# Dealing out the x products of a block by columns: 320, fourteen times 290, and 324 a step

## The chip, the cores and the metric

The kernel runs on one core of one Trainium2 chip. The metric is the time of one execution in device microseconds; for the kernel before, three runs were taken.

## The reference

The kernel computes a gated recurrence over 512 time steps for a batch of 8, with 512 inputs and 512 hidden units, and adds its input:

```python
def step(h, x_t):
    fused = jax.nn.sigmoid(jnp.concatenate([x_t, h], axis=-1) @ w_W + w_b)
    hidden_state, output_state = jnp.split(fused, 2, axis=-1)
    memory_state = x_t @ wx_W + wx_b + hidden_state * (h @ wh_W + wh_b)
    h_new = output_state * h + (1.0 - output_state) * jnp.tanh(memory_state)
    return (h_new, h_new)
_, hs = jax.lax.scan(step, h0, xT)
x = x + swapaxes(hs, 0, 1)
```

Each step needs the h of the step before. The parts that multiply x_t do not depend on h; they can be computed ahead for many steps at once. Everything is float32.

## The kernel before

**Steps.** One loop runs over the 512 steps. In each step TensorE first multiplies h, in the order `A0 A1 A2 A3 D0 D1 D2 D3 H2 H3` (`ORDER`): a letter is a PSUM bank (A 256 columns, D 128, H 64), a digit is one of four chunks of 128 hidden units. A2 and A3 use 192 of A's columns. For each of them four matmuls of 32 output columns go to four strips of the array (`j`, partitions 32j to 32j + 31). All matmuls go through the helper `mm`, so their line in the profile is always L203. The state h lies in `hT`, in two halves: chunks 0 and 1, and chunks 2 and 3.

When A is complete, VectorE transposes the gates out of it (`turn_r`, whose tile is `tr`, L523, then `turn_h`, `turn_z`, `turn_part`), ScalarE applies the sigmoids and the tanh, and VectorE's scans (L511) form the memory state `m` and, in `update`, the new `hT`: first the half that A0 and A1 of the next step read, then the half that A2 and A3 read. VectorE also has three short memsets on `idle` to settle its order.

**The x side.** The 512 steps make 32 blocks of 16 (`TC`). The x part of the first two blocks is computed directly (`prefill`). From the third block on it comes out of a two-level fast multiplication, which needs 49 products a block instead of 64: seven stages `STAGES` of seven products. Each product is `BL` = 96 columns wide, with four `mm` for the four strips; each `mm` is recorded in the trace as two matmuls with two weight loads. The stationary operand is a 128 x 32 piece of x or of sums of x (`xin`, `so`, `si`), the moving one a 96-column piece of weights or of differences of weights (`wx`, `tw`, `ti`).

A stage puts three products side by side into PSUM bank `xps[0]` (columns 0 to 287) and four into `xps[1]` (0 to 383); `SLOTS` says which. When a bank is complete in a stage, VectorE adds it to earlier sums (`drain`, L403), and the next stage writes that bank again, in some stages accumulating on what stands there. GpSimd adds up the results (`result`) and also forms the sums of x.

**What sets the order.** All orders are written out by hand (`manual_schedule`): instructions of an engine run in the order in which the Python code emits them. `products` is a generator that yields after each product, `x_side` chains it over blocks 2 to 31, and the loop over steps advances it with `take` right after the matmuls of H, so the x products of a step stand between H of this step and A0 of the next. `LEAD` = 18 makes the products of block c run from step 16c - 18 on. The number of products per step is in

```python
take(later, 4 if (i + LEAD) % TC == TC - 1 else 3)
```

which gives 15 steps of three and one of four: 49. A second loop, ahead of the steps, counts the same numbers (`done += 3 + w // 15`) and lists for each step the drains of the banks that are complete by then; VectorE runs them at the end of that step, after the updates. The last 18 steps have no x products.

Of the kernel before, what the change touches and what calls it, by code (L numbers as in the profile page):

```python
# [14 lines left out]
NQ = 4  # L15
# [19 lines left out]
BL = 96  # L35
# [3 lines left out]
FRESH = (2, 5, 1)  # L39

SLOTS = ((1, 6, 7), (2, 3, 4, 5))

LEAD = 18

PLAIN = (2, 3, 5, 6, 8, 10, 11, 13, 14, 16)

# [8 lines left out]
def tile_cond_rnn_residual(  # L55
# [144 lines left out]
    xps = [psum.tile([P, 512], F32, name=f"xp{q}") for q in range(2)]  # L200

    def mm(out_, lhsT, rhs, start=False):
        nc.tensor.matmul(  # L203
            out_, lhsT, rhs, start=start, stop=False, skip_group_check=True
        )
# [20 lines left out]
    for b in range(2):  # L226
        c0 = COLS.start + BL * b
# [56 lines left out]
    def wx_of(kh, nh):  # L284
        return wx[:, 2 * kh : 2 * kh + 2, :, HALF * nh : HALF * nh + HALF]
# [31 lines left out]
    def x_block(c, r, kh):  # L317

        return xins[c][:, :, 2 * kh : 2 * kh + 2, 32 * r : 32 * r + 32]
# [31 lines left out]
    def x_sums(c):  # L351
        jobs = [(x_sum, c, n) for n in range(4)]
        return jobs + [(inner_x, c, n, p) for n in range(4) for p in (0, 2, 3)]

    def left(c, p, q):

        xr, kh = {1: (0, 0), 2: (0, 1), 4: (1, 1)}.get(p, (None, None))
        at = {1: 0, 2: 1, 4: 2, 5: 3, 6: 4, 7: 5, 3: 6}[p]
        if q in (3, 5, 6, 7):
            return si[c % 2][:, at, {5: 0, 6: 1, 7: 2, 3: 3}[q]]  # L360
        e, k = {1: (0, 0), 2: (0, 1), 4: (1, 1)}[q]
        if xr is None:
            return so[c % 2][:, at - 3, e, k]
        return x_block(c, xr, kh)[:, e, k]

    def right(p, q, j):

        kh, nh = {1: (0, 0), 2: (1, 0), 3: (1, 1)}.get(p, (None, None))
        at = {1: 0, 2: 1, 3: 2, 5: 3, 6: 4, 7: 5, 4: 6}[p]
        if q > 3:  # L370
            return ti[:, at, {5: 0, 6: 1, 7: 2, 4: 3}[q], j]
        k, b = {1: (0, 0), 2: (1, 0), 3: (1, 1)}[q]
        w = tw[:, at - 3] if kh is None else wx_of(kh, nh)
        return w[:, k, j, BL * b : BL * b + BL]

    def products(c):

        for q in STAGES:
            for bank in range(2):
                for n, p in enumerate(SLOTS[bank]):  # L380
                    for j in range(NQ):
                        mm(
                            xps[bank][32 * j : 32 * j + 32, BL * n : BL * n + BL],
                            left(c, p, q),
                            right(p, q, j),
                            start=q in FRESH and n == 0,
                        )
                    yield

    def drain(q, bank):  # L390

# [28 lines left out]
    def take(it, n=None):  # L420
        while n is None or n > 0:
            if next(it, it) is it:
                return
            n = None if n is None else n - 1

    def x_side():
        for c in range(2, NCH):
            yield from products(c)
# [4 lines left out]
    later = x_side()  # L433
# [13 lines left out]
    def at_step(i, *todo):  # L447
        jobs.setdefault(i, []).extend(todo)
# [7 lines left out]
    for c in range(2, NCH):  # L456
        w0 = TC * c - LEAD
        for n, q in enumerate(x_sums(c)):
            at_step(w0 - (13 if c > 2 else 10) + n // 2, q)
        done = 0  # L460
        for w in range(TC):
            n = done
            done += 3 + w // 15
            for m, q in enumerate(STAGES):
                for bank in range(2):
                    if n < 7 * m + 3 + 4 * bank <= done:
                        drains.setdefault(w0 + w, []).append((q, bank))
        for e, w in ((0, 11), (1, 15)):
            for n in range(7):
                at_step(w0 + w + n // 2, (result, e, n))  # L470

    pool_done = {}
    for i in range(T):
        g, s = divmod(i, GS)
        c, t = divmod(i, TC)
# [6 lines left out]
        for n in (ORDER if i else FIRST).split():  # L482
# [3 lines left out]
            bank, k = n[0], int(n[1])  # L486
# [10 lines left out]
        if 1 <= i < 4:  # L497
            take(first[2], 2 if i == 3 else 3)
        elif i == 0:
            take(first[1], 1)  # L500
        elif i < 4 + len(PLAIN):
            take(first[4], PLAIN[i - 4] - (PLAIN[i - 5] if i > 4 else 0))
        else:
            take(later, 4 if (i + LEAD) % TC == TC - 1 else 3)

        rows = slice(B * s, B * s + B)
        s1 = (i + 1) % GS
# [253 lines left out]
```

## Time and profile before

| | |
|---|---|
| median of three runs | 1645.9 us (1644.61 to 1647.66) |
| the profiled execution | 1646.05 us, span 1644.0 us |
| PE busy | 1628.2 us, 53006 matmuls |
| PEld busy | 1360.1 us, 53006 weight loads |
| DVE busy | 1379.4 us |
| ACT busy | 976.8 us |
| POOL busy | 569.3 us |
| mean granted TensorE clock | 1.000 |

How to read it: the span goes from the first to the last instruction of one profiled execution. PE is TensorE's matmuls, PEld its weight loads, which overlap with matmuls; DVE is VectorE, ACT ScalarE, POOL GpSimd. The end of a matmul is modelled, so a busy PE isn't PE at its peak. In a timeline row stand the start, the duration, the engine, the line, the operation, out<-in, the shape and the count of merged instructions, and in brackets the idle time of the engine before it with what ended it. In a row of windows stand the stretch, its length, and for PE, PEld, DVE, ACT and POOL the busy time and count, then the granted clock, the DMA share and GB/s. In a row of waits stand the total, the number and the longest, in microseconds. In a group by shape stand the busy time in us and the mean of one instruction in ns.

### The profile page before, as it was taken

How to read it: one execution, taken by the hardware profiler on the slowest of the kernel's cores; microseconds unless marked ns; L12 is line 12 of the kernel's file. 1: busy time of each engine (PE TensorE's matmuls, PEld its weight loads, DVE VectorE, ACT ScalarE, POOL GpSimd, SP SyncE). 2: the span in 40 equal slices, each digit the busy share in tenths (PEclk: the TensorE clock that was granted, in tenths of full speed). 3: DMA queues.
4: the chain of work that ended last, by engine and by line, in shares of the span. 5: the costliest groups of instructions: out<-in, count | busy, mean ns of one | idle time of the engine just before them, and what ended most of it. 6: DMA issues, size and time to landing. Idle time of an engine off the chain costs nothing.

```text
span 1644.0 us, 124813 instructions
## 1 busy us (share of the span) xinstructions
PE 1628.2 (99%) x53006; PEld 1360.1 (83%) x53006; DVE 1379.4 (84%) x11215; ACT 976.8 (59%) x5520; POOL 569.3 (35%) x1467
## 2 busy tenths in 40 slices
PE   8999999999999999999999999999999999999998
PEld 4788888888888888888888888888888888888876
DVE  8688888888888888888888888888888888888886
ACT  3666656556555656666656656655655566666665
POOL 7433333333333333333333333333333333333220
PEclk9999999999999999999999999999999999999999
DMA  4000000000000000000000000000000000000000
GB/s 181 11 10 18 18 18 17 6 18 17 18 18 5 18 18 18 18 17 5 18 18 18 18 5 18 18 18 17 18 5 18 18 18 18 5 18 11 12 11 10
DMA packets 11512, 31.08 MB, mean 19 GB/s; under 512 B 1220, under 2 KB 1732, under 8 KB 10952
## 3 DMA queue, kind: packets, MB, share of 16 engines
q1 hardware_dynamic: 10800, 22.94, 4.1%
q8 instruction: 414, 6.78, 1.7%
q14 instruction: 146, 1.20, 0.2%
q10 hardware_dynamic: 152, 0.16, 0.0%
HBM read 14.70 MB, written 8.39 MB: 14 GB/s over the span
## 4 chain that ended last, share of the span: by engine, by line
PE 97%; DVE 2%; POOL 1%; DMA 0%; issue 0%; ACT 0%; DVEq 0%; POOLq 0%
PE A L203 48%; PE D L203 26%; PE xp L203 16%; PE H L203 7%; DVE tr L523 0%; DVE m L511 0%; POOL ti L315 0%; DMA rows<-in_bias_dram 0%; DVE hT L511 0%; POOL xs L225 0%; DVE md1B L580 0%; DVE md1A L538 0%; DVE tz L523 0%; POOL off L229 0%; DVE tw L296 0%
## 5 line engine op out<-in xcount | busy, mean ns | idle before, releaser
L203 PE MATMUL A<-wa,hT 128*32 128x256 f32 x16352 | 885.9, 356 | 5.7 <-DVE hT L511 5.2
L203 PEld LDWEIGHTS A<-wa,hT 128*32 128x32 f32 x16352 | 507.7, 123 | 241.4 <-DVE hT L511 138.9
L203 PE MATMUL D<-wd,hT 128*32 128x128 f32 x16384 | 543.1, 273 | 1.0 <-DMA wd<-in_wd_dram 1.0
L203 PEld LDWEIGHTS D<-wd,hT 128*32 128x32 f32 x16384 | 482.8, 122 | 21.7 <-DMA wd<-in_wd_dram 1.3
L675 POOL TENSOR_TENSOR ot<-xin,hT 128x32 f32<-128x32 f32 x503 | 132.3, 263 | 1047.3 <-DVE hT L511 1035.9
L243 ACT ACTIVATE hT<-m 128x8 f32<-128x8 f32 x2048 | 324.4, 207 | 98.0 <-DVE m L511 97.7
L243 ACT ACTIVATE md0A<-tr 128x16 f32<-128x16 f32 x512 | 112.9, 220 | 407.3 <-DVE tr L523 407.3
L523 DVE STREAM_TRANSPOSE tr<-A 128x64 f32<-128x64 f32 x511 | 127.7, 250 | 229.1 <-PE A L203 229.1
L243 ACT ACTIVATE hT<-hT 128x16 f32<-128x16 f32 x1024 | 233.1, 228 | 85.0 <-DVE hT L511 84.2
L203 PE MATMUL H<-wa,hT 128*32 128x64 f32 x8208 | 210.3, 219 | 0.0
L203 PEld LDWEIGHTS H<-wa,hT 128*32 128x32 f32 x8208 | 187.5, 122 | 0.0
L511 DVE TENSOR_TENSOR_SCAN hT<-hd0A,hT 128x24 f32<-128x24 f32 x1024 | 176.3, 172 | 0.0
L511 DVE TENSOR_TENSOR_SCAN hT<-hd0B,hT 128x24 f32<-128x24 f32 x1024 | 154.4, 192 | 21.8
L511 DVE TENSOR_TENSOR_SCAN m<-md0B,md1B 128x24 f32<-128x24 f32 x1024 | 154.5, 192 | 0.0
L203 PE MATMUL xp<-ti,si 128*32 128x96 f32 x5040 | 150.1, 246 | 0.2 <-issue 0.2
L511 DVE TENSOR_TENSOR_SCAN m<-md0A,md1A 128x16 f32<-128x16 f32 x1024 | 144.2, 182 | 5.1
L243 ACT ACTIVATE md0B<-tr 128x16 f32<-128x16 f32 x512 | 116.2, 227 | 42.2 <-DVE tr L523 0.5
L418 POOL TENSOR_TENSOR xs<-ff 128x192 f32<-128x192 f32 x240 | 140.6, 596 | 0.2
L580 DVE STREAM_TRANSPOSE md1B<-A 128x64 f32<-128x64 f32 x511 | 130.0, 254 | 0.0
L243 ACT ACTIVATE hd0A<-tz 128x16 f32<-128x16 f32 x512 | 116.6, 228 | 21.4
L538 DVE STREAM_TRANSPOSE md1B<-H 128x64 f32<-128x64 f32 x512 | 127.8, 250 | 0.0
L573 DVE STREAM_TRANSPOSE hd0B<-sz 128x64 f32<-128x64 f32 x512 | 126.4, 247 | 0.0
(103 smaller groups left out, 1924.4 us busy)
## 6 DMA issues: line engine op xcount, KB each, us to landing
xin<-in_x_dram SPq DMA_DIRECT2D x31, 256.0 KB, 3.3
out_dram<-ot SPq DMA_DIRECT2D x31, 256.0 KB, 2.2
wx<-in_wx_dram SPq DMA_DIRECT2D x4, 768.0 KB, 7.1
wa<-in_wa_dram SPq DMA_DIRECT2D x4, 512.0 KB, 9.7
wd<-in_wd_dram SPq DMA_DIRECT2D x1, 768.0 KB
wd<-in_wd_dram SPq DMA_DIRECT2D x1, 256.0 KB, 11.2
out_dram<-ot SPq DMA_DIRECT2D x1, 192.0 KB, 1.8
head<-in_xh_dram ACTq DMA_DIRECT2D x1, 144.0 KB, 5.1
```

What stands on the lines that cost most here:

```text
L203: nc.tensor.matmul(out_, lhsT, rhs, start=start, stop=False, skip_group_check=True)
L243: inst = nc.scalar.activation(out_, in_, func, **kw).ins
L418: nc.gpsimd.tensor_tensor(to, a, b, ALU.add)
L511: return nc.vector.tensor_tensor_scan(*[t_[:, :, c_].rearrange("p n c s -> p (n c s)") for t_ in (out_, d0, d1)], 0.0, ALU.mult, ALU.add,).ins
L523: inst = nc.vector.transpose(t_.rearrange("p c n -> p (c n)"), raw[n][hf]).ins
L538: inst = nc.vector.transpose(md1[hf][g % 2][:, :, :, hf].rearrange("p n c -> p c n"), raw["h"][hf]).ins
L573: inst = nc.vector.transpose(hd0[1][i % 2][:, :, :, 2].rearrange("p n c -> p c n"), sz).ins
L580: nc.vector.transpose(md1[1][g % 2][:, :, :, 0].rearrange("p n c -> p c n"), ps["A"][:, :HU])
L675: pool_done[i + 1] = nc.gpsimd.tensor_tensor(ot[:, t], x_of(c, slice(0, NQ), t, 1), hTs[(i + 1) % NH][:, :, :, B * s1 : B * s1 + B, 2].rea ...
```

## The change

The x products are no longer dealt out in whole products but in columns. A block has 49 x 96 = 4704 columns; `BURSTS` gives 320 to the first step of a block, 290 to each of the next fourteen, and 324 to the last. Where a burst ends inside a product, the product is divided: its first columns are multiplied in this step and the rest in the next, with the same stationary operand loaded again. A divided product that opens a bank marks only its first piece as the start. The generator now yields after each burst, so a step takes one. The list of drains counts columns instead of products.

```diff
+BURSTS = (320,) + (290,) * 14 + (324,)
...
     def products(c):
 
+        todo = list(BURSTS)
         for q in STAGES:
             for bank in range(2):
                 for n, p in enumerate(SLOTS[bank]):
-                    for j in range(NQ):
-                        mm(
-                            xps[bank][32 * j : 32 * j + 32, BL * n : BL * n + BL],
-                            left(c, p, q),
-                            right(p, q, j),
-                            start=q in FRESH and n == 0,
-                        )
-                    yield
+                    c0 = 0
+                    while c0 < BL:
+                        c1 = min(BL, c0 + todo[0])
+                        for j in range(NQ):
+                            mm(
+                                xps[bank][32 * j : 32 * j + 32, BL * n + c0 : BL * n + c1],
+                                left(c, p, q),
+                                right(p, q, j)[:, c0:c1],
+                                start=q in FRESH and n == 0 and c0 == 0,
+                            )
+                        todo[0] -= c1 - c0
+                        c0 = c1
+                        if not todo[0]:
+                            todo.pop(0)
+                            yield
...
-            done += 3 + w // 15
+            done += BURSTS[w]
             for m, q in enumerate(STAGES):
                 for bank in range(2):
-                    if n < 7 * m + 3 + 4 * bank <= done:
+                    if n < BL * (7 * m + 3 + 4 * bank) <= done:
                         drains.setdefault(w0 + w, []).append((q, bank))
...
-            take(later, 4 if (i + LEAD) % TC == TC - 1 else 3)
+            take(later, 1)
```

## The prediction

> **What bounds the kernel now.** The page first: its span, its busy line and the instruction queue; then the waits of the whole run.
>
> ```profile
> span 1644.0 us, 124813 instructions
> PE 1628.2 (99%) x53006; PEld 1360.1 (83%) x53006; DVE 1379.4 (84%) x11215; ACT 976.8 (59%) x5520; POOL 569.3 (35%) x1467
> PEld A L203 <- DVE hT L511: 138.9, 489, 1.4
> DVE tr L523 <- PE A L203: 229.1, 510, 1.5
> ```
>
> PE is busy 99%, which looks like a TensorE-bound kernel. The two waits say otherwise: 489 times, about once in each of the 512 steps, the weight load of A waits for the scan that makes hT, and 510 times VectorE waits for A. Two engines that wait for each other once a step form a loop, and either side of it can set the pace. So I read one step of three products in the timeline, from one transpose `tr` (VectorE's first work once A is complete) to the next.
>
> ```profile
> 801.55 1.06 PE L203 MATMUL D<-wd,hT 128*32 128x128 f32 x32
> 801.80 0.25 DVE L523 STREAM_TRANSPOSE tr<-A 128x64 f32<-128x64 f32 x1 [0.31 <-PE A L203]
> 802.42 0.41 PE L203 MATMUL H<-wa,hT 128*32 128x64 f32 x16
> 802.65 0.35 PE L203 MATMUL xp<-wx,xin 128*32 128x96 f32 x8
> 802.81 0.51 PE L203 MATMUL xp<-tw,so 128*32 128x96 f32 x16
> 803.14 1.73 PE L203 MATMUL A<-wa,hT 128*32 128x256 f32 x32
> 803.74 0.20 DVE L511 TENSOR_TENSOR_SCAN hT<-hd0B,hT 128x24 f32<-128x24 f32 x1
> 804.00 0.51 PEld L203 LDWEIGHTS A<-wa,hT 128*32 128x32 f32 x16 [0.28 <-DVE hT L511]
> 804.94 0.25 DVE L523 STREAM_TRANSPOSE tr<-A 128x64 f32<-128x64 f32 x1 [0.41 <-PE A L203]
> ```
>
> VectorE starts at 801.80 and its scan of the second half of hT ends at 803.94; 0.06 us later the load for the last half of A goes out, having sat idle 0.28 us; A then needs until 804.94. The x products run from 802.65 to 803.14, while PE would otherwise wait for VectorE. They are filler, and they cost time only once they are longer than the hole.
>
> How deep the hole is shows in the windows over fifteen steps of three products, one step of four, and sixteen steps near the end that have no x products at all; under them the same windows for the tile xp, then the starts of `tr` that I used as borders, then the steady stretch of thirty blocks.
>
> ```profile
> 779.87:826.87 47.00, 47.00 (x1572) 39.52 (x1565) 39.99 (x328) 28.30 (x161) 16.53 (x44) 1.00 0.05 16
> 826.87:830.14 3.27, 3.27 (x124) 2.89 (x117) 2.78 (x22) 1.93 (x11) 0.87 (x4) 1.00 0.02 5
> 1585.69:1635.72 50.03, 46.19 (x1292) 35.39 (x1285) 36.54 (x333) 29.82 (x170) 7.50 (x22) 1.00 0.04 13
> ...
> 1585.69:1635.72 50.03, 0.00 (x0) 0.00 (x0) 0.00 (x0) 0.00 (x0) 1.00 0.04 13
> ...
> 779.87 0.25 DVE L523 STREAM_TRANSPOSE tr<-A 128x64 f32<-128x64 f32 x1 [0.44 <-PE A L203]
> 826.87 0.25 DVE L523 STREAM_TRANSPOSE tr<-A 128x64 f32<-128x64 f32 x1 [0.41 <-PE A L203]
> 830.14 0.25 DVE L523 STREAM_TRANSPOSE tr<-A 128x64 f32<-128x64 f32 x1 [0.44 <-PE A L203]
> 1585.69 0.25 DVE L523 STREAM_TRANSPOSE tr<-A 128x64 f32<-128x64 f32 x1 [0.44 <-PE A L203]
> 1635.72 0.25 DVE L523 STREAM_TRANSPOSE tr<-A 128x64 f32<-128x64 f32 x1 [0.88 <-PE A L203]
> ...
> 74.26:1585.69 1511.43, 1510.98 (x50172) 1278.76 (x50165) 1283.03 (x10501) 908.86 (x5160) 513.37 (x1359) 1.00 0.05 15
> ```
>
> Three products: 47.00 / 15 = 3.133 us a step. Without x products: 50.03 / 16 = 3.127 us, the same within 6 ns though a sixth of PE's work is missing. So the step of three products goes at the pace of the loop through VectorE. Four products: 3.27 us, and PE is the slower side there:
>
> ```profile
> 828.30 1.41 PEld L203 LDWEIGHTS A<-wa,hT 128*32 128x32 f32 x32
> ```
>
> all 32 loads of A in one row, with no wait for hT. A block of sixteen steps thus takes 15 x 3.133 + 3.270 = 50.265 us. Thirty such blocks are 1507.9 us; the steady stretch has 1511.43, so 3.5 us go to other stalls (below).
>
> **What a column and a split cost PE.** The mean duration of one matmul by shape:
>
> ```profile
> L203 PE MATMUL H<-wa,hT 128*32 128x64 f32 x8208 | 210.3, 219 | 0.0
> L203 PE MATMUL xp<-wx,xin 128*32 128x384 f32 x192 | 17.9, 486 | 0.0
> ```
>
> (486 - 219) / 320 = 0.834 ns a column. One product is eight recorded matmuls (the 802.65 row), that is, two passes of four strips that run side by side. A step of four products has 28 passes: A eight (four of 256 and four of 192 columns), D eight of 128, H four of 64, x eight of 96, 3840 columns together. 3840 x 0.834 = 3.203 us; the 0.067 us missing to 3.27 are 2.4 ns a pass. So a pass of n columns takes 0.834 n + 2.4 ns, a piece of a product two passes, and a split by itself 4.8 ns, if its weights arrive in time. Three products: 3648 columns and 26 passes, 3.105 us. The hole has 3.133 - 3.105 = 0.028 us left, and four products miss it by 0.137 us.
>
> **The change, part by part.** Columns per block stay 4704. The borders between steps fall 32, 34 and so on to 60 columns into a product, never on its edge, so a block has 15 pieces more: 450 in thirty blocks. Every burst consists of four pieces.
>
> - First step, 320 columns: 32 columns and one piece more, 53.4 + 4.8 = 58 ns, PE 3.163 us: 30 ns longer than 3.133.
> - Fourteen steps of 290: 3.3 + 4.8 = 8 ns, PE 3.113 us, still 20 ns inside the hole: nothing. What hides them is the wait for the hT scan; without that cover they would cost 14 x 8 = 114 ns a block.
> - Last step, 324 columns: 36 columns and one piece more than three products, 65 ns, PE 3.170 us instead of 3.270: 100 ns gained.
>
> Sum: 70 ns a block, 2.1 us in thirty.
>
> No other engine's order changes. Stage ends lie at columns 288, 672, 960 and so on, and each falls into the same step as before, so every drain keeps its step and none meets another. A bank 1 is written again 288 columns after its last drain point; a burst of 290 could overrun that only if it began one column ahead of a stage end, and all borders are even. So PE gets no new wait for a drain that is late. SP, ScalarE and GpSimd issue what they did.
>
> **Short pieces.** A pass cannot be shorter than the loading of the next weights. The shortest passes now are H's 64 columns: four in 802.42 to 802.65, 57 ns each, near the formula's 56, so a load fits into 56. The new pieces have 32 to 64 columns, down to 29.1 ns. Nearest to a bound from below is the load that came late, cut off by two windows that end 10 ns apart:
>
> ```profile
> 804.00 0.14 PEld L203 LDWEIGHTS A<-wa,hT 128*32 128x32 f32 x4 [0.28 <-DVE hT L511]
> 804.00 0.17 PEld L203 LDWEIGHTS A<-wa,hT 128*32 128x32 f32 x5 [0.28 <-DVE hT L511]
> ```
>
> At 804.03 four loads have started, at 804.04 a fifth: the second set follows the first by 30 to 40 ns. I take 35, since this is a load as fast as it goes, and H only shows that it isn't slower than 56. Passes under 35 ns are those under 39 columns. In the middle steps the 20 ns of room cover them (34 columns: 2 x (35 - 30.8) = 8). The first step pays 2 x (35 - 29.1) = 12 ns for its piece of 32, the last 2 x (35 - 32.4) = 5 for its piece of 36. That takes 17 of the 70 ns: 53 a block, 1.6 us.
>
> The Trainium skill, page "TensorE: Matmul & The Clock Gate", section "LDWEIGHTS (loading the stationary operand)", puts a load at its number of columns divided by 1.2 GHz, 27 ns for 32 columns. By it, no piece would be short of weights and the sum would stay at 2.1 us; the trace's 30 to 40 ns are above it, and I go by the trace.
>
> **More instructions to fetch.** From the page and from the waits of the weight loads in the window 75 to 1586:
>
> ```profile
> q8 instruction: 414, 6.78, 1.7%
> PEld A L203 <- issue: 1.2, 2, 0.6
> PEld xp L203 <- issue: 0.6, 2, 0.4
> ```
>
> 6.78 MB over 106,012 PE records are 64 bytes each, so q8 feeds PE. The 450 pieces add 16 records each, 7200, 6.8%: 28 more packets. In the steady stretch four waits, 1.8 us, have no releaser but issue; I take them, and the rest of the 3.5 us, for late fetches. In proportion they grow by 0.24 us. A packet comes every 1644 / 414 = 3.97 us and then every 3.72, so each late one is 0.25 us later: 1 us for four. Bounds 0 and 2 (half of 3.5 more); I take 0.4.
>
> Together: -1.6 + 0.4 = -1.2 us. The profiled execution took 1646.05 us (2.05 outside its span, untouched); it comes to 1644.85. It lies 0.15 above the median of the runs, which goes from 1645.9 to 1644.7 us. That is 0.07%; a measurement of this kernel tells about 0.2%, 3.3 us, from no change, so this is a forecast of no measurable difference.
>
> **Rivals.**
>
> Short pieces hold PE up (slower). If a pass needs 56 ns whatever its columns, each middle step has a leading and a trailing piece, 98 columns together, and pays 2 x (112 - 86.5) = 51 ns: 3.164 us, 31 over the loop, fourteen times. First step 3.217 (84 more than now), last 3.217 (53 less). 434 + 84 - 53 = 465 ns a block, +13.9 us: 1659.8. At 45 ns a pass the change breaks even; at 50 the middle steps pay 9 ns on average, first and last +72 and -65, 139 ns a block, +4.2 us: 1650.1. It decides from just under 50 ns. For it: nothing shorter than 56 was ever sustained here. Against: the 30 to 40 ns above. Chance 0.22.
>
> Everything fits (faster). If PE's sums for the two ends were too high and all sixteen steps ran at 3.133, 137 ns a block go, 4.1 us: 1641.8. The late fetches can help too: their 3.5 us may fall elsewhere when packets meet other steps. Against: the formula leaves 30 and 37 ns in the two ends. With the scatter of three runs (1644.61 to 1647.66) 0.20.
>
> The change doesn't do what it says: PE sets the pace in the steps of three as well, so evening out gains nothing and 450 splits cost 4.8 ns each, +2.2 us: 1648.1. The stretch without x products speaks against it. Chance 0.05. Late fetches at their upper bound with the rest as forecast, 1646.3: 0.10, also without measurable difference.
>
> **How the numbers follow.** The forecast itself has 0.43; its own range is 1643.5 (nothing for short pieces or fetches, and some scatter) to 1646.5. The rival of short pieces lies beyond 3.3 us slower in all of its 0.22, and scatter and late fetches add 0.04: slower 0.26. Faster 0.20 is the rival alone. Same: 0.43 + 0.05 + 0.10 less the 0.04, 0.54. The range for 8 in 10 runs from 1642.2, near the fastest case, to 1652, a pass of some 51 ns.
>
> **What would show it.** In the profile after: fourteen of sixteen `tr` to `tr` distances at 3.13 us; 3.16 to 3.18 in the two ends, no 3.27; weight loads of A still waiting for hT some 480 times, with a shorter total; matmuls of xp from 32 columns up whose group starts lie at 0.834 n + 2.4 ns a pass, not under about 35; DVE, ACT and POOL counts unchanged; q8 near 442 packets. Passes of 50 ns or more for short pieces, middle steps above 3.14, or many more issue waits would prove it wrong.

## The result, and the profile after

The changed kernel takes 1700.21 us (median of four runs, 1691.68 to 1706.29) against 1646.45 before: a ratio of 1.0319 (95% interval 1.03 to 1.0338), 3.2% slower. The forecast was 1644.7 us, no measurable difference.

The page of the changed kernel; its profiled execution took 1695.39 us:

```profile
span 1693.2 us, 132013 instructions
PE 1662.4 (98%) x56606; PEld 1432.5 (85%) x56606; DVE 1385.3 (82%) x11215; ACT 976.9 (58%) x5520; POOL 570.5 (34%) x1467
q8 instruction: 442, 7.24, 1.8%
```

The counts are as worked out: 3600 more matmuls and as many loads, 28 more packets on the instruction queue, nothing new on DVE, ACT and POOL. Busy time on DVE grew by 6 us only. What grew is time in which PE has nothing to do. The waits of the weight loads in the window 75 to 1630 (total, times, longest), and under them those for hT in the kernel before, window 75 to 1586:

```profile
PEld A L205 <- DVE hT L521: 89.2, 360, 0.6
PEld xp L205 <- issue: 21.7, 55, 0.6
PEld A L205 <- issue: 8.2, 21, 0.6
PEld H L205 <- issue: 4.0, 13, 0.5
PEld D L205 <- issue: 1.8, 8, 0.3
...
PEld A L203 <- DVE hT L511: 120.9, 442, 0.4
```

Before, issue (a wait for nothing that the profile shows) stood behind four loads and 1.8 us in the steady stretch; now behind 97 loads and 35.7 us, and not in front of the divided xp products alone but also of A, H and D, whose instructions did not change. The waits for hT have become fewer, 360 instead of 442. A wait that also strikes tiles whose instructions are unchanged doesn't look like a wait for the data of divided products. The timeline of the weight loads, in a bad stretch:

```profile
770.68 0.27 PEld L205 LDWEIGHTS H<-wa,hT 128*32 128x32 f32 x8
771.40 0.19 PEld L205 LDWEIGHTS H<-wa,hT 128*32 128x32 f32 x8 [0.46 <-issue]
...
774.62 0.18 PEld L205 LDWEIGHTS xp<-wx,xin 128*32 128x32 f32 x8
775.15 0.16 PEld L205 LDWEIGHTS xp<-wx,so 128*32 128x32 f32 x8 [0.34 <-issue]
...
778.89 0.15 PEld L205 LDWEIGHTS xp<-ti,si 128*32 128x32 f32 x7 [0.31 <-issue]
...
782.91 0.94 PEld L205 LDWEIGHTS A<-wa,hT 128*32 128x32 f32 x23 [0.61 <-DVE hT L521]
```

and the windows from the end of one of these gaps to the end of the next (length, then busy time and count of PE, PEld and the others):

```profile
771.39:775.14 3.75, 3.54 (x128) 2.93 (x128) 2.87 (x24) 2.01 (x13) 0.90 (x3) 1.00 0.02 4
775.14:778.89 3.75, 3.65 (x128) 3.05 (x128) 2.54 (x25) 2.04 (x13) 0.75 (x3) 1.00 0.02 7
778.89:782.91 4.02, 3.84 (x128) 3.26 (x128) 3.32 (x28) 2.19 (x13) 0.97 (x3) 1.00 0.01 4
```

128 matmuls and 128 loads lie between two gaps, each time. 256 recorded instructions of 64 bytes are 16 KB, one packet of q8. (The last gap is put down to hT, but it falls on the same count of 256; part of it at least is of the same kind.) Counted record by record, all 97 issue waits of the window stand at one place in the count: the load that waits is number 92 of each 128 near the start and number 78 near the end, moving evenly and never more than half a load off. (A few instructions of PE that aren't among the records would explain the movement; that isn't shown.) The four waits of the kernel before stand at the same place to within a load. PE stops where a packet of its program ends and goes on 3.75 to 4.02 us after it last went on. That gives the theory: **PE's program arrives no faster than one packet in some 3.7 us**, whatever the instructions do. A step before had 208 recorded PE instructions, 208 / 256 x 3.7 = 3.01 us, hidden under the loop's 3.133; the change makes it 224, which need 3.24 us, and that no longer fits (both times are estimates from the 3.7 us).

The steady stretch gives the mean. In thirty blocks of the changed kernel, from the `tr` of step 14 to that of step 494:

```profile
74.31:1634.61 1560.30, 1543.75 (x53772) 1351.09 (x53765) 1288.50 (x10501) 908.75 (x5160) 514.60 (x1358) 1.00 0.05 15
```

53772 + 53765 records are 420.1 packets, 3.71 us each. Before, by the row of that stretch, 50172 + 50165 records in 1511.43 us were 391.9 packets, 3.86 us each: only 4% above 3.71, and the change asked for 7% more instructions.

### The profile page after: what moved, and what is told of

Read it like the earlier page. It is cut to its first block, busy times and chain, and to the rows that moved or that the text cites. A ratio compares the mean times of both kernels' runs of the same rounds, so it can differ in the third digit from the quotient of the medians.

```text
span 1693.2 us, 132013 instructions
## 1 busy us (share of the span) xinstructions
PE 1662.4 (98%) x56606; PEld 1432.5 (85%) x56606; DVE 1385.3 (82%) x11215; ACT 976.9 (58%) x5520; POOL 570.5 (34%) x1467
## 4 chain that ended last, share of the span: by engine, by line
PE 96%; DVE 2%; issue 1%; POOL 1%; ACT 0%; DVEq 0%; POOLq 0%
PE A L205 47%; PE D L205 25%; PE xp L205 16%; PE H L205 7%; DVE tr L533 0%; DVE m L521 0%; POOL ti L317 0%; DVE hT L521 0%; DVE md1B L590 0%; DVE md1A L548 0%; DVE tz L533 0%; POOL xs L227 0%; POOL off L231 0%; DVE tw L298 0%; DVE md1B L548 0%
## 5 line engine op out<-in xcount | busy, mean ns | idle before, releaser
L205 PE MATMUL A<-wa,hT 128*32 128x256 f32 x16352 | 907.5, 356 | 7.8 <-DVE hT L521 5.2
L205 PEld LDWEIGHTS A<-wa,hT 128*32 128x32 f32 x16352 | 560.7, 124 | 195.1 <-DVE hT L521 107.9
L205 PE MATMUL D<-wd,hT 128*32 128x128 f32 x16384 | 565.4, 273 | 1.1 <-DMA wd<-in_wd_dram 0.9
L205 PEld LDWEIGHTS D<-wd,hT 128*32 128x32 f32 x16384 | 504.7, 122 | 18.2 <-issue 1.8
L205 PE MATMUL H<-wa,hT 128*32 128x64 f32 x8208 | 235.2, 219 | 2.2 <-issue 1.9
L205 PEld LDWEIGHTS H<-wa,hT 128*32 128x32 f32 x8208 | 208.4, 122 | 4.5 <-issue 4.0
L205 PE MATMUL xp<-ti,si 128*32 128x96 f32 (+12 forms) x6480 | 166.2, 229 | 3.7 <-issue 3.2
L205 PEld LDWEIGHTS xp<-ti,si 128*32 128x32 f32 x6480 | 136.6, 110 | 6.5 <-issue 6.0
```

The lines of the kernel that those rows point to most:

```text
L205: nc.tensor.matmul(out_, lhsT, rhs, start=start, stop=False, skip_group_check=True)
```

## The experiments

Theory 1 is the supply of instructions, theory 2 that the divided or short products cost the time themselves, by their passes or by their waits. The kernels ran on three chips, each beside runs of the kernel before: D0 divided, the change with a merged H, half a packet and three divided products a block beside 19 runs (median 1645.87 us); those of 240, 216 and 192 and the one with A0 divided beside 13 (1646.54); one divided product a block beside 15 (1646.23). In brackets stand the ratio to the kernel before on the same chip and its 95% interval.

**As many instructions without any divided product** (the kernel before, changed in the loop over `ORDER`):

```diff
-            for j in range(NQ):
-                mm(to[32 * j : 32 * j + 32, :], hs, w_[:, k, j])
+            w = to.shape[1]
+            halves = ((0, w // 2), (w // 2, w)) if bank == "D" and k == 0 and 14 <= i < 494 else ((0, w),)
+            for u0, u1 in halves:
+                for j in range(NQ):
+                    mm(to[32 * j : 32 * j + 32, u0:u1], hs, w_[:, k, j, u0:u1])
```

> The kernel before, whole x products, but in steps 14 to 493 the D0 matmuls are issued as two halves of 64 columns: 16 more recorded PE instructions a step (208 becomes 224), 4.8 ns more of PE work, nothing shorter than 64 columns. Theory 1, instruction supply (PE gets 256 recorded instructions, one 16 KB packet, no faster than about every 3.75 us, so a step of 224 needs 3.28 us against a loop of 3.13): as slow as the changed kernel, 1685 to 1715 us, with long gaps on PE at packet borders. Theory 2, the short and divided x products themselves are slow: no change, 1645 to 1649 us.

Measured: 1707.31 us (1.0376, 1.0359 to 1.0393). The x products are those of the kernel before, and the time is that of the change or a little more. Theory 2 falls here: no divided product is needed for the slowdown. The window over its steady stretch:

```profile
74.02:1645.97 1571.95, 1554.59 (x54008) 1352.31 (x54001) 1296.35 (x10500) 907.88 (x5160) 513.82 (x1359) 1.00 0.05 15
```

**The change with 16 instructions fewer.** H2 and H3, two matmuls of 64 columns per strip, become one of 128:

```diff
-BANKS = {"A": 256, "D": 128, "H": 64}
+BANKS = {"A": 256, "D": 128, "H": 128}
...
+            one = bank == "H" and 14 <= i < 494
+            if one and k == 3:
+                continue
...
-                "H": (ps["H"], wa[:, :, :, :64]),
+                "H": (ps["H"], wa[:, :, :, :128]) if one else (ps["H"][:, :64], wa[:, :, :, :64]),
```

> The changed kernel with all its divided products, but in steps 14 to 493 H2 is one matmul of 128 columns per strip and H3 is left out: the same PE columns, 16 recorded PE instructions fewer a step (224 becomes 208). H3's share of the sum is left out. Theory 1, instruction supply: the stalls go and the gain first forecast shows, 1643 to 1647 us. Theory 2, divided products are slow in themselves or wait for drains: still about 1700 us.

Measured: 1641.75 us (0.9976, 0.9967 to 0.9985), 58 us below the changed kernel with all its divided products in place, and below the range expected. All waits of its weight loads in the window 75 to 1586:

```profile
PEld A L205 <- DVE hT L524: 126.1, 483, 0.4
```

The window over its steady stretch:

```profile
74.65:1581.06 1506.41, 1506.41 (x49932) 1273.07 (x49924) 1283.53 (x10501) 908.90 (x5160) 513.59 (x1358) 1.00 0.05 15
```

One kind of wait is left, the one for hT, and not one issue. This kernel also shows what the rest of the prediction was worth. Its timeline of PE in a first step of a block:

```profile
828.81 0.51 PE L205 MATMUL xp<-tw,so 128*32 128x96 f32 x16
829.14 0.24 PE L205 MATMUL xp<-wx,xin 128*32 128x32 f32 x8
829.20 1.06 PE L205 MATMUL A<-wa,hT 128*32 128x256 f32 x16
```

The timeline of DVE at the `tr` starts around that first step and around a last one:

```profile
827.80 0.25 DVE L536 STREAM_TRANSPOSE tr<-A 128x64 f32<-128x64 f32 x1 [0.34 <-PE A L205]
830.99 0.25 DVE L536 STREAM_TRANSPOSE tr<-A 128x64 f32<-128x64 f32 x1 [0.45 <-PE A L205]
874.85 0.25 DVE L536 STREAM_TRANSPOSE tr<-A 128x64 f32<-128x64 f32 x1 [0.41 <-PE A L205]
878.02 0.25 DVE L536 STREAM_TRANSPOSE tr<-A 128x64 f32<-128x64 f32 x1 [0.33 <-PE A L205]
```

The piece of 32 columns takes 829.14 to 829.20, two passes of 30 ns; it is 60 ns in each of the thirty blocks. First step 3.19 us here and last 3.17 (means over thirty blocks 3.18 and 3.17; forecast 3.175 for both), and the thirty blocks take 1506.41 us where the forecast's 50.212 a block makes 1506.36. That the two agree to 0.05 us is partly luck: the merged H also saves two passes a step, by the forecast's formula 4.8 ns in the first and in the last step, 0.3 us in thirty blocks.

**Half a packet of other instructions ahead of the loop** (in the changed kernel):

```diff
     mm(xps[1], zeros[:, :128], zeros, start=True)
+    for _ in range(32):
+        mm(xps[1][:, :8], zeros[:, :128], zeros[:, :8])
```

> The changed kernel with 32 matmuls of 8 zero columns ahead of the loop, 128 recorded PE instructions, half a packet. A step has 224 instructions, seven eighths of a packet, so packet borders fall at the same place of a step every eight steps; half a packet moves them by four steps. Theory 1, instruction supply: the slow steps, in the change the burst numbers 0, 1, 2 and 8, 9, 10 of a block, become 4, 5, 6 and 12, 13, 14; total again 1690 to 1710 us. Theory 2, the cost sits in certain pieces or stages: the slow steps stay where they are.

Measured, one run: 1723.83 us, above the range, because the 32 matmuls weren't hidden: step 14 begins at 89.10 us instead of 74.31. Without these 14.8 us it is 1709.0. Mean step in us by its number in the block, counted from step 14 on and worked out from the starts of `tr` in all thirty blocks:

```
step in block     0    1    2    3    4    5    6    7    8    9   10   11   12   13   14   15
before         3.13 3.13 3.13 3.21 3.14 3.13 3.14 3.13 3.14 3.13 3.13 3.14 3.14 3.13 3.14 3.27
changed        3.39 3.34 3.41 3.14 3.13 3.16 3.21 3.23 3.39 3.37 3.34 3.14 3.14 3.15 3.19 3.29
shifted        3.18 3.15 3.15 3.55 3.46 3.49 3.28 3.16 3.14 3.16 3.16 3.22 3.39 3.44 3.38 3.18
```

The slow steps were 0 to 2 and 8 to 10 and are now 3 to 5 and 12 to 14, half a period on (3 to 4 steps, where 4 were expected), though each step has the same pieces as before. The period is eight steps, since 224 is seven eighths of 256. Why some steps are slow and others not can be estimated: from one border to the next are one step and 32 records more, 16 matmuls. Sixteen of H take 0.23 us (802.42 to 802.65 in the kernel before), so PE would be at the next border after 3.133 + 0.23 = 3.36 us and must wait for a packet that takes 3.7. Sixteen of A with 256 columns take by the formula four passes of 216 ns, 0.86 us; PE is there after 3.99 us and the packet has come.

**How the cost grows with the count.** D0 and D1 divided as D0 was above (240 a step), D0 divided only in even steps (216), A0 divided instead of D0 (224, with the new instructions among the longest matmuls), and the kernel before with the merged H of the second experiment (192; H3's share left out). The conditions in `halves` are

```text
240: bank == "D" and k < 2 and 14 <= i < 494
216: bank == "D" and k == 0 and 14 <= i < 494 and i % 2 == 0
224: bank == "A" and k == 0 and 14 <= i < 494
```

> The kernel before with D0 and D1 issued as two halves of 64 columns in steps 14 to 493: 240 recorded PE instructions a step, 10 ns more PE work. Theory 1, instruction supply at about 3.7 to 3.8 us per 256: 240 of them need 3.47 to 3.56 us a step against 3.14, so 480 steps cost 160 to 200 us more: 1805 to 1850 us. Rival, only the place of a packet border in the step matters and supply in total is enough: a cost like that of 224, about 1700 us, or less.

> The kernel before with D0 issued as two halves of 64 columns in every second step of 14 to 493: 216 recorded PE instructions a step on average. Theory 1, instruction supply: 216 need 3.13 to 3.2 us, just at the loop's 3.133, so the onset: 1648 to 1675 us. Rival, cost in proportion to added instructions (61 us for 16 a step): 1676 us.

> The kernel before with A0, the longest matmul, issued as two halves of 128 columns in steps 14 to 493: 224 recorded PE instructions a step as in the change, but the 16 more lie among long matmuls, not among short ones. Theory 1 as a matter of the mean rate: 1690 to 1715 us. Rival, only the density of instructions around the short matmuls matters: under 1660 us.

> The kernel before with H2 as one matmul of 128 columns per strip and H3 left out in steps 14 to 493: 192 recorded PE instructions a step, the same PE columns. H3's share of the sum is left out. Theory 1, instruction supply: the 3.5 us of stalls that the kernel before still has go, its pace of 15 x 3.133 + 3.265 stays: about 1642.5 us, so that the dealing out by columns, which gave 1641.75 at 208 instructions, is worth only 1 to 2 us. Rival, the kernel before has no stalls of supply: 1645.9 us, and all 4 us of that run came from the dealing out.

Measured: 1803.01 us for 240 (1.0952, 1.093 to 1.0974), 1657.91 for 216 (1.0068, 1.0051 to 1.0085), 1693.07 for A0 (1.0284, 1.0263 to 1.0304), 1644.31 for 192 (0.9988, 0.9979 to 0.9997). The first three speak for theory 1: 240 a hair under its range of 1805 to 1850, far above a cost that depends on the border's place alone; 216 at the onset, below the proportional 1676; A0 inside 1690 to 1715 and far from the rival's 1660, so the count decides in the main. Whether the place of the instructions adds something stays open: with the same count, A0 divided is 14 us faster than D0 divided, but the two ran on different chips, and the four runs of the changed kernel alone are 14.6 us apart. The steady stretch of 240:

```profile
74.55:1743.76 1669.21, 1607.58 (x57848) 1396.45 (x57841) 1312.03 (x10500) 913.78 (x5160) 514.15 (x1359) 1.00 0.05 14
```

of 216:

```profile
75.13:1597.94 1522.81, 1519.54 (x52088) 1298.22 (x52081) 1286.15 (x10500) 914.84 (x5160) 514.21 (x1359) 1.00 0.05 15
```

with A0 divided:

```profile
74.02:1632.27 1558.25, 1545.20 (x54004) 1391.33 (x53997) 1289.25 (x10501) 915.04 (x5160) 514.00 (x1359) 1.00 0.05 15
```

and of 192:

```profile
74.06:1583.17 1509.11, 1509.11 (x46332) 1268.13 (x46326) 1283.91 (x10500) 914.39 (x5160) 514.06 (x1359) 1.00 0.05 15
```

Records divided by 256, and the length by that: 3.69 us a packet at 240, 3.74 at 216, 3.69 with A0 divided, 3.73 with D0 divided, 3.71 in the change, 3.75 with half a packet ahead of the loop (53774 + 53766 records in 1574.36 us), 3.86 before and in the second experiment, 4.17 at 192. Wherever PE is short of program, the packet costs about the same 3.7 us, and at 208 a step and below the loop decides.

The kernel of 192 came out 2.2 us under the one before, not the 3.4 expected, and 1.8 us above its 1642.5; still under the rival's 1645.9. Its steady stretch is 2.3 us shorter than before, so most, not all, of the 3.5 us of other stalls was supply. That fits the kernel before: 2.2 us of them lie in four single steps of 3.40 to 3.86 us, all of them number 3 of their blocks, and that number has 3.14 us in the kernel of 192.

**Fewer divided products, all of the work kept.** Twelve steps of 288 and then four that share the rest; and fourteen of 288 with 336 twice:

```diff
-BURSTS = (320,) + (290,) * 14 + (324,)
+BURSTS = (288,) * 12 + (320, 300, 300, 328)
```

> The changed kernel with other bursts: 288 columns in the first twelve steps of a block, then 320, 300, 300 and 328, so that only three products a block are divided (3392 recorded PE instructions a block, against 3344 before and 3584 in the change). PE's own work by 0.834 ns a column and 2.4 ns a pass: 3.163, 3.130, 3.130, 3.177 us in the last four steps, against 3.133 three times and 3.270: 63 ns a block less, 1.9 us. Theory 1, instruction supply: 212 instructions a step on average stays within 256 per 3.75 us, but the last four steps have 224, so some stalls: 1643 to 1649 us. Theory 2, a divided product costs by itself (54 us for 450 of them, 0.12 us each): 90 of them, 1656 us.

```diff
-BURSTS = (320,) + (290,) * 14 + (324,)
+BURSTS = (288,) * 14 + (336, 336)
```

> The changed kernel with bursts of 288 in fourteen steps and 336 in the last two: one divided product a block, 3360 recorded PE instructions (3344 before). PE's work in the last two steps 3.19 us each, against 3.133 and 3.27 before: 23 ns a block, 0.7 us less. Theory 1, instruction supply: two steps in a row of 224 instructions instead of one may give a few more stalls; 1645 to 1648 us, no difference that can be measured, and no version that keeps all the work gets to the 1642 us seen with 16 instructions fewer. Rival, an even load is what counts and a few divided products are free: 1645.2 us or less.

Measured: 1648.36 us (1.0015, 1.0005 to 1.0024) with three divided products a block, 1646.27 (0.9999, 0.999 to 1.0008) with one. Even three in a block give back more than the 1.9 us that they gain on PE, and one gains nothing that shows; its interval, 1.6 us down to 1.3 us up, doesn't shut out the 0.7 us that the rival forecast. Theory 2's price of 0.12 us for each divided product (1656) fails again.

No version that computes everything beat the kernel before. The second experiment suggests what it would take: the columns dealt out as in the change, and 16 recorded PE instructions fewer a step from somewhere. I found no place for that which doesn't put work ahead of a bank that VectorE waits for.

## Why the prediction was wrong

**The step that failed** is "More instructions to fetch". It foresaw the 7200 records and the 28 packets, and it priced them at 0.4 us with 2 as the upper bound. Measured: the steady stretch of the changed kernel is 1560.30 us, 53.9 above the 1506.4 that its pace without stalls makes, against 3.5 before. The term was 50 us. I treated late packets as four accidents that grow in proportion. They were the first signs of a floor. The 3.97 and 3.72 us a packet that I compared are means over the whole run, and the start and the last 18 steps thin them out. In the steady stretch the forecast's 50.212 us a block for 14 packets ask for one every 3.59 us, and 3.71 on average, with 3.75 to 4.02 in a row of gaps, is what PE gets: 14 x 30 times the 0.12 to 0.13 us between them is the loss. The trace of before doesn't hold the floor, but it holds a bound that I didn't draw: its steady row gives 3.86 us a packet, with some stalls already. Taken as full at that pace, the change's 16 x 224 / 256 = 14 packets a block need 54.0 us instead of 50.2, 114 us more in thirty blocks. That would have been the upper end, not 2 us; the measured 50 lies between. The rival "late fetches at their upper bound" ended at 1646.3 for the same reason.

**What bounds the kernel** held. The loop through VectorE sets 3.133 us; with enough program the middle steps ran at it in spite of 290 columns (3.13 to 3.14 in the second experiment's means).

**Columns and splits** held: 0.834 n + 2.4 ns a pass and 4.8 ns a split gave 3.163 to 3.175 us for the first step, and 3.18 was measured; 3.175 for the last, and 3.17.

**Short pieces** held, and the slower rival built on them fell. A pass of 32 columns takes about 30 ns, nearer to the formula's 29 than to the 35 taken, and far from the just under 50 from which that rival would decide. It had the right side, slower, by the wrong mechanism, and that is luck.

**The gain of dealing out by columns**, forecast at 1.6 to 2.1 us, agrees with the runs as far as they can tell. Between the second experiment (0.9976) and the kernel of 192 (0.9988), both free of issue waits, it is 0.12% of 1646, 2.0 us, and 2.7 us between their steady stretches; the two ran on different chips and their intervals overlap. The other 2 us by which the second experiment beats the kernel before came with the merged H, as the kernel of 192 shows.

**The order of the other engines** held: the same counts, and no new wait for a drain among the waits.

The Trainium skill, page "Runtime: NRT & Kernel Launch", section "Instruction fetch mechanics", says that an engine's program is refilled in blocks of 16 KiB, 256 instructions, and that crossing a block is mostly hidden. The trace agrees on the block: 128 matmuls and 128 loads between gaps. It disagrees on the second point for this kernel, where 420 crossings in the steady stretch cost 54 us, 0.13 us each.

What stays open is why a packet takes 3.7 us, but the trace narrows it. The DMA views of the changed kernel for 771.40 to 775.15 and for 778.90 to 782.92, from one going on of PE to the next, have (the digit marks the fortieth of the window in which a packet starts; under it packets, MB, share of 16 engines)

```profile
DMA  0000000000000006000000000000000000000000
q8 instruction: 1, 0.02, 1.6%
...
DMA  0000000000000000500000000000000000000000
q8 instruction: 1, 0.02, 1.4%
```

In each window there is one packet. It starts 1.4 to 1.5 us and 1.6 to 1.7 us after PE went on, its transfer takes 3.75 x 16 x 1.6% = 0.96 us and 4.02 x 16 x 1.4% = 0.9 us, and PE goes on again some 1.3 to 1.5 us after its end. Counted at all 97 issue waits, the last packet had ended 1.2 to 1.6 us before PE went on (median 1.42), and the next started 1.0 to 1.7 us after (median 1.17). So the transfer is a quarter of the time. The rest is two delays before and behind it, with one packet at a time, and the three together make about the 3.7 us. That the next packet is asked for only when PE crosses a border fits this, but the asking itself isn't in the trace, and no run separates asking, fetching and using.

## What to carry to other kernels

Count the instructions of the densest engine, not its columns: divide the records of a steady stretch by 256 and its length by that, and compare the time a packet with the lowest one that a run has shown. Take the stretch where the work is densest: a mean over the whole run (3.72 us here) can hide that the stretch asks for more (3.59) than it gets. When a change adds instructions to an engine that already has unexplained issue waits, price the addition as if that supply were full. An experiment that adds the same count of instructions elsewhere, without the change itself, tells whether the count or the content costs.

## What the runs showed of the hardware

PE got its program at 3.69 to 3.75 us for 256 recorded instructions (matmuls and weight loads, 64 bytes each) in every kernel here with 216 or more of them a step, about 14.5 ns an instruction on average; in the change, issue waits of up to 0.6 us stand at a fixed count of 256. In the two windows whose DMA view is shown, one 16 KB packet was fetched from one going on of PE to the next, and its transfer took a quarter of the time. Float32 matmuls of 32 output columns on four strips, with two recorded matmuls and two loads for each, run much faster than that while they are at hand: a pass of eight records took 30 ns at 32 moving columns, under 4 ns each. So it isn't the rate at which PE can start instructions that sets the 14.5 ns.
